# Levels 1 and 3 cross attention of a four-level Perceiver: scores stored negated by the operation that finds their maximum, turned probabilities of a unit in two banks

## The chip, the cores and the metric

The kernel is one program on one core of a Trainium2 chip. The time is what the device takes for one execution, in microseconds (us). The core has TensorE (PE; its weight loads are listed as PEld), VectorE (DVE), ScalarE (ACT), GpSimd (POOL) and SyncE (SP), each with its own queue of instructions; they wait for each other by semaphores. Matrix products write to PSUM, which the kernel divides into eight banks of 128 x 512 numbers of 4 bytes. Everything here is in float32.

## What is computed

The reference runs four levels over `x` (2 batches of 64 rows, 256 features). Each level has a cross attention to a context of 2 x 1024 rows with 192 features, a second mixing block, and a mixture of experts. The change is in the cross attention of levels 1 and 3, which have the same core (level 3 goes on with a two-layer product instead of `Wo`):

```python
q = (query @ Wq + bq).reshape(B, Nq, NUM_HEADS, HEAD_DIM).transpose(0, 2, 1, 3)
k = (key @ Wk + bk).reshape(B, Nk, NUM_HEADS, HEAD_DIM).transpose(0, 2, 1, 3)
v = (value @ Wv + bv).reshape(B, Nk, NUM_HEADS, HEAD_DIM).transpose(0, 2, 1, 3)
attn = jnp.einsum('bhqd,bhkd->bhqk', q, k) * SCALE
attn = jax.nn.softmax(attn, axis=-1)
out = jnp.einsum('bhqk,bhkd->bhqd', attn, v)
```

Here B = 2, Nq = 64, Nk = 1024, 16 heads of 16 features. The query is the normalized `x`, so each level's attention waits for everything before it; keys and values come from the context and are made ahead.

## The kernel before

The program goes level by level. `narrow_attention` (L1277) does the attention of levels 1 and 3. Its work is cut into 16 **units**. A unit is one batch `b`, one half `c` of the features (8 heads) and one pair `t` of heads: its scores have 128 rows (2 heads x 64 queries) and 1024 columns (keys). Four units with the same `b` and `c` make a **group** `g`. The function walks through 8 **rounds** `r` of two units, `mine = 2r` and `other = 2r + 1`.

A unit goes through these steps:

- `scores` (L1307): four products in all for the two units of a round; each unit's scores fill two neighbouring PSUM banks (`two_banks`).
- `largest` (L1320): DVE finds the negated maximum of each row (L1322), straight from PSUM.
- `exponentials` (L1324): ACT computes exp(score - maximum) from PSUM into the SBUF tile `p` and sums each row (L1328).
- `turn` (L1333): PE transposes `p`, four blocks of 128 x 128 for each half `k` of the keys (L1343), into one bank.
- `take` (L1349): the bank is copied to the SBUF tile `pT`, by ACT (L1352) or DVE (L1354). Of the four banks of a round, ACT takes three and DVE the last.
- `weigh` (L1364): for the group before, PE multiplies V with the turned probabilities of all four units, the half `k` = 0 in even rounds and 1 in odd ones (L1369); in even rounds it also transposes the reciprocal row sums, which DVE (`rinv`, L1359) and POOL (`wide`, L1361) have spread.
- `first_half`, `second_half`, `heads_of`: DVE takes the product out of its bank (`part`, L1381 and L1386), POOL masks it, and DVE scales it and puts the two heads together (`own`, `n_oT`).

Two things set when a step can run. First, the whole stage stands under `in_written_order` (L274): PE, DVE, ACT and POOL each run their instructions in the order in which the function writes them. Second, there are few buffers. PSUM is split by `psum(3, 2)`: three pairs of banks, from which `two_banks()` hands out one, and two single banks, from which `bank()` does. A new tile waits until the last reader of the buffer that it gets is done. Before the change, pairs hold scores only, and are free when the exponential has read them; single banks hold turned probabilities and the product of `weigh`, five uses in a round. `p` has three buffers, `pT` one or two for each of the eight pieces of a group.

The part of a round that is rewritten is this (L1415 to L1428):

```python
exponentials(other)
if more:
    scores(r + 1)
ps = turn(mine, 0)
take(mine, 0, ps, nc.scalar)
ps = turn(mine, 1)
if more:
    largest(mine + 2)
take(mine, 1, ps, nc.scalar)
if g >= 0:
    po = weigh(g, k, wide)
if more:
    exponentials(mine + 2)
```

After it come `turn(other, 0)`, `largest(other + 2)`, the half of `part`, the two copies of `other` and, in odd rounds, `heads_of`. Before the loop, the stage makes the queries, the scores of units 0 and 1, the last pieces of the keys, and the first maxima and the first exponential. After it, the last group is multiplied.

Of the kernel before, what the change touches and what calls it, by code (L numbers as in the profile page):

```python
# [8 lines left out]
F32 = mybir.dt.float32  # L9
U8 = mybir.dt.uint8  # L10
U32 = mybir.dt.uint32
AF = mybir.ActivationFunctionType
ALU = mybir.AluOpType
AX = mybir.AxisListType
# [3 lines left out]
P = 128  # L18
# [3 lines left out]
NK = 1024  # L22
# [35 lines left out]
def tile_perceiver(ctx: ExitStack, tc: tile.TileContext, i: dict, out: bass.AP):  # L58
    nc = tc.nc
# [30 lines left out]
    def two_banks():  # L90
        return psum_now["a"].tile([P, 1024], F32, tag="a", name="two_banks")

    def stat(n=1, name="stat"):
        return small.tile([P, n], F32, tag=f"s{n}", bufs=12 if n == 1 else 4, name=name)

    turn = [0]
# [65 lines left out]
    ident = const.tile([P, P], F32, name="ident")  # L162
# [640 lines left out]
    with psum(2, 4), stage_pool(name="l0x", bufs=1) as pool, stage_pool(  # L803
        name="l0x_prep", bufs=2
# [189 lines left out]
        sc, p, rinv, pT, u, uT = {}, {}, {}, {}, {}, {}  # L994
# [84 lines left out]
        ps = bank()  # L1079
# [28 lines left out]
        a, b, c, d = ((b, j) for b in range(NB) for j in range(2))  # L1108
# [165 lines left out]

    def narrow_attention(pool, att, x, wq, bq, bv, kv, gap, tail=()):  # L1277
        qx = pool.tile([P, 2, 2, NB, 2, S], F32, name="n_qx")
        oT = pool.tile([P, 2, P], F32, name="n_oT")
        kT, v = kv.kT, kv.v  # L1280
        bq_own = stat(8, "bq_own")
        at = COL[bq][0]
        for h in range(2):
            nc.vector.tensor_scalar(
                bq_own[:, 4 * h : 4 * h + 4], cols[:, at : at + 4], quarter[:, h : h + 1],
                None, ALU.mult,
            )
        units = [(b, c, t) for b in range(NB) for c in range(2) for t in range(4)]
        rounds = len(units) // 2
        sc, p, total, pT, part = {}, {}, {}, {}, {}  # L1290

        def queries(ps, c):

            for n in range(2):
                for h in range(2):
                    dst = qx[:, c, n, :, h, :]
                    src = ps[:, n * P : (n + 1) * P].rearrange("p (b q) -> p b q", b=NB)
                    one, k = quarter[:, h : h + 1], 2 * c + n
                    if n == 0:
                        nc.vector.tensor_scalar(dst, src, col(bq, k), one, ALU.add, ALU.mult)  # L1300
                    else:
                        nc.scalar.activation(
                            dst, src, AF.Identity, bias=bq_own[:, 4 * h + k : 4 * h + k + 1],
                            scale=one,
                        )

        def scores(r):  # L1307
            for u in (2 * r, 2 * r + 1):
                b, c, t = units[u]
                sc[u] = two_banks()  # L1310
                for n in range(2):
                    rows_ = 32 * ((t + 2 * n) % 4)
                    rows_ = slice(rows_, rows_ + 32)
                    nc.tensor.matmul(  # L1314
                        sc[u][:, n * 512 : (n + 1) * 512],
                        qx[rows_, c, n, b].rearrange("p h q -> p (h q)"), kT[c, b][rows_, n, :],
                        start=True, stop=True,
                    )

        def largest(u):  # L1320
            sc[u] = sc[u], stat(name="negmax")
            nc.vector.tensor_reduce(sc[u][1], sc[u][0], AX.X, ALU.max, negate=True)  # L1322

        def exponentials(u):  # L1324
            if u % 4 == 0:
                total[u // 4] = stat(4, "total")
            p[u] = att.tile([P, NK], F32, tag="p", name="p")
            nc.scalar.activation(  # L1328
                p[u], sc[u][0], AF.Exp, bias=sc[u][1], scale=1.0,
                accum_out=total[u // 4][:, u % 4 : u % 4 + 1],  # L1330
            )

        def turn(u, k):  # L1333


            t = u % 4
            pT[u, k] = att.tile(
                [P, 4, P], F32, tag=f"pT{t}{k}", bufs=1 if 2 * k + 1 <= t else 2,
                name="pT",
            )  # L1340
            ps = bank()
            for kc in range(4):
                nc.tensor.transpose(  # L1343
                    ps[:, kc * P : (kc + 1) * P],
                    p[u][:, (4 * k + kc) * P : (4 * k + kc + 1) * P], ident,
                )
            return ps

        def take(u, k, ps, engine):  # L1349
            dst = pT[u, k].rearrange("p c t -> p (c t)")  # L1350
            if engine is nc.scalar:
                nc.scalar.copy(dst, ps)  # L1352
            else:
                nc.vector.tensor_copy(dst, ps)  # L1354

        def spread(g):

            rinv = stat(4, "rinv")
            nc.vector.reciprocal(rinv, total[g])  # L1359
            wide = att.tile([P, 4, 32], F32, tag="wide", bufs=2, name="wide")  # L1360
            nc.gpsimd.tensor_copy(wide, rinv.unsqueeze(2).to_broadcast([P, 4, 32]))  # L1361
            return wide

        def weigh(g, k, wide=None):  # L1364
            b, c, _ = units[4 * g]
            po = bank()
            for kc in range(4 * k, 4 * k + 4):
                for t in range(4):
                    nc.tensor.matmul(  # L1369
                        po[32 * t : 32 * t + 32, :P],  # L1370
                        v[:, b, kc // 4, kc % 4, c * P + 32 * t : c * P + 32 * t + 32],
                        pT[4 * g + t, k][:, kc % 4, :], start=(kc == 4 * k), stop=(kc == 4 * k + 3),
                    )
            if k == 0:

                nc.tensor.transpose(po[:, P : 2 * P], wide.rearrange("p t d -> p (t d)"), ident)
            return po

        def first_half(g, po):
            part[g] = att.tile([P, 2 * P], F32, tag="part", bufs=2, name="part")  # L1380
            nc.vector.tensor_copy(part[g], po[:, : 2 * P])  # L1381
            own = part[g][:, P:]
            nc.gpsimd.tensor_tensor(own, own, parity, ALU.mult)

        def second_half(g, po):
            nc.vector.tensor_tensor(part[g][:, :P], po[:, :P], part[g][:, :P], ALU.add)  # L1386

        def heads_of(g):
            b, c, _ = units[4 * g]
            own = att.tile([P, P], F32, tag="own", bufs=2, name="own")  # L1390
            nc.vector.tensor_tensor(own, part[g][:, :P], part[g][:, P:], ALU.mult)

            nc.vector.scalar_tensor_tensor(
                oT[:, c, b * S : (b + 1) * S], own[:, :S], col(bv, c), own[:, S:],
                ALU.add, ALU.add,
            )

        with in_written_order():
            steps(gap, 3)
            xlT = turned_rows(layernorm(x, then=AF.Exp))  # L1400
            ps = [features(xlT, wq, 2 * c, 2) for c in range(2)]
            queries(ps[0], 0)
            scores(0)
            queries(ps[1], 1)
            steps(gap)
            largest(0)
            exponentials(0)
            largest(1)
            for r in range(rounds):
                g, k = r // 2 - 1, r % 2  # L1410
                mine, other = 2 * r, 2 * r + 1
                more = r + 1 < rounds
                if g >= 0 and k == 0:
                    wide = spread(g)
                exponentials(other)  # L1415
                if more:
                    scores(r + 1)
                ps = turn(mine, 0)
                take(mine, 0, ps, nc.scalar)
                ps = turn(mine, 1)  # L1420
                if more:
                    largest(mine + 2)
                take(mine, 1, ps, nc.scalar)
                if g >= 0:
                    po = weigh(g, k, wide)
                if more:
                    exponentials(mine + 2)
                ps = turn(other, 0)  # L1428
                if more:
                    largest(other + 2)  # L1430
                if g >= 0:
                    (second_half if k else first_half)(g, po)
                take(other, 0, ps, nc.scalar)
                ps = turn(other, 1)
                take(other, 1, ps, nc.vector)
                if g >= 0 and k:
                    heads_of(g)
            g = rounds // 2 - 1
            wide = spread(g)
            first_half(g, weigh(g, 0, wide))  # L1440
            second_half(g, weigh(g, 1))
            steps(tail, 1)
            heads_of(g)
            steps(tail)
        return oT
# [931 lines left out]
```

## Time and profile before

The time is 718.98 us, the median of three runs (718.66 to 720.44).

| what | value |
|---|---|
| span of the profiled execution | 719.9 us |
| time of the profiled execution | 721.7 us |
| granted PE clock over it, mean | 0.976 |
| PE busy | 663.7 us (92%) |
| PEld busy | 514.3 us (71%) |
| DVE busy | 300.7 us (42%) |
| ACT busy | 262.4 us (36%) |
| POOL busy | 65.6 us (9%) |
| L1343, transposes of `p`: 256 of them | 39.7 us busy |
| L1322, maxima: 32 | 37.6 us busy, 1216 ns each |
| L1328, exponentials: 32 | 36.1 us busy, 1127 ns each |
| L1352, copies by ACT: 48 | 27.0 us busy, 588 ns each |
| level 1 attention, first scores to the last step of `n_oT` | 151.7 to 198.0 us |
| level 3 attention, the same | 577.7 to 622.6 us |

In the rows of the profile, a line such as L1343 is the kernel's line, then come the engine, the operation, the tile written and the tiles read, the shape as partitions x elements, and how often. Times are from the start of the span. What stands in brackets, or behind the second bar, is how long the engine sat idle before, and what ended that. The clock is the share of full speed that TensorE was granted.

### The profile page before, as it was taken

How to read it: one execution, taken by the hardware profiler on the slowest of the kernel's cores; microseconds unless marked ns; L12 is line 12 of the kernel's file. 1: busy time of each engine (PE TensorE's matmuls, PEld its weight loads, DVE VectorE, ACT ScalarE, POOL GpSimd, SP SyncE). 2: the span in 40 equal slices, each digit the busy share in tenths (PEclk: the TensorE clock that was granted, in tenths of full speed). 3: DMA queues.
4: the chain of work that ended last, by engine and by line, in shares of the span. 5: the costliest groups of instructions: out<-in, count | busy, mean ns of one | idle time of the engine just before them, and what ended most of it. 6: DMA issues, size and time to landing. Idle time of an engine off the chain costs nothing.

```text
span 719.9 us, 11877 instructions
## 1 busy us (share of the span) xinstructions
PE 663.7 (92%) x4916; PEld 514.3 (71%) x4916; DVE 300.7 (42%) x757; ACT 262.4 (36%) x541; POOL 65.6 (9%) x93
## 2 busy tenths in 40 slices
PE   7789979989979999999998989999999989779997
PEld 3456657955659998899997678999979856543543
DVE  5854443147650003555553435534331367543111
ACT  2453252258653242322222415305131278432111
POOL 3520100000100000000000030220000000000240
PEclk9999999989999999999999999999999999969999
DMA  9940011850005887100000400020148800447981
GB/s 285 422 170 1 1 51 54 307 195 1 2 2 189 302 284 278 59 1 2 1 1 30 147 0 1 3 80 39 59 150 305 301 5 2 162 204 283 376 335 66
DMA packets 21226, 92.81 MB, mean 129 GB/s; under 512 B 3043, under 2 KB 7669, under 8 KB 12373
## 3 DMA queue, kind: packets, MB, share of 16 engines
q1 hardware_dynamic: 18896, 85.70, 32.7%
q0 software_dynamic: 2016, 6.30, 2.4%
q8 instruction: 39, 0.64, 0.4%
q14 instruction: 15, 0.12, 0.0%
q10 hardware_dynamic: 260, 0.06, 0.0%
HBM read 98.20 MB, written 0.13 MB: 137 GB/s over the span
## 4 chain that ended last, share of the span: by engine, by line
PE 84%; DVE 9%; ACT 4%; issue 2%; DMA 0%; POOL 0%; DVEq 0%; ACTq 0%; POOLq 0%
PE bank L261 29%; PE bank L1642 6%; PE two_banks L590 5%; PE two_banks L1591 4%; PE bank L1343 4%; PE two_banks L1314 3%; PE bank L635 3%; PE two_banks L1598 2%; PE bank L1369 2%; PE two_banks L1837 2%; PE bank L1957 2%; PE two_banks L405 1%; PE two_banks L379 1%; PE two_banks L261 1%; PE bank L1945 1%
## 5 line engine op out<-in xcount | busy, mean ns | idle before, releaser
L1642 PE MATMUL bank<-l2x_ctx,p 128*128 128x193 f32 x256 | 48.1, 327 | 0.0
L354 DVE SCALAR_TENSOR_TENSOR x_new<-bank,comb,x_new 128x256 f32<-128x256 f32 x24 | 11.6, 484 | 79.7 <-PE bank L261 79.7
L1343 PEld LDWEIGHTS bank<-ident,p 128*128 128x128 f32 x256 | 29.9, 150 | 18.5 <-issue 7.8
L1642 PEld LDWEIGHTS bank<-l2x_ctx,p 128*128 128x128 f32 x256 | 40.8, 191 | 0.4
L1343 PE MATMUL bank<-ident,p 128*128 128x128 f32 x256 | 39.7, 299 | 1.3 <-ACT pT L1352 0.5
L1322 DVE TENSOR_REDUCE negmax<-two_banks 128x1 f32<-128x1024 f32 x32 | 37.6, 1216 | 7.2 <-PE two_banks L1314 7.2
L1328 ACT ACTIVATE p<-two_banks,negmax 128x1024 f32<-128x1024 f32 x32 | 36.1, 1127 | 0.8 <-DVE negmax L1322 0.8
L1352 ACT COPY pT<-bank 128x512 f32<-128x512 f32 x48 | 27.0, 588 | 14.6 <-PE bank L1343 14.6
L1591 PE MATMUL two_banks<-l2x_qA,ctxA 128*128 128x128 f32 x256 | 31.9, 278 | 0.0
L261 PEld LDWEIGHTS bank<-xT,l1f_w_sb 128*128 128x128 f32 x256 | 31.3, 201 | 0.6 <-issue 0.3
L261 PE MATMUL bank<-xT,l1f_w_sb 128*128 128x128 f32 x256 | 31.7, 285 | 0.0
L1591 PEld LDWEIGHTS two_banks<-l2x_qA,ctxA 128*128 128x128 f32 x256 | 30.3, 192 | 1.1 <-issue 1.0
L1532 ACT ACTIVATE l1f_hT<-bank,cols 128x128 f32<-128x128 f32 x64 | 18.3, 368 | 34.4 <-PE bank L261 34.4
L1606 DVE TENSOR_REDUCE l2x_mx<-two_banks 128x128 f32<-128x1024 f32 x16 | 19.6, 1225 | 26.5 <-PE two_banks L1598 26.5
L261 PEld LDWEIGHTS bank<-xT,l2f_w_sb 128*128 128x128 f32 x256 | 29.6, 192 | 0.3
L261 PE MATMUL bank<-xT,l2f_w_sb 128*128 128x128 f32 x256 | 29.8, 275 | 0.0
L261 PE MATMUL bank<-l1f_w_sb,l1f_hT 128*128 128x256 f32 x128 | 28.8, 379 | 0.0
L1314 PE MATMUL two_banks<-n_kT,n_qx 32*128 32x512 f32 x128 | 25.1, 677 | 2.8 <-ACT n_kT L450 1.8
L1628 DVE TENSOR_TENSOR p<-two_banks,l2x_shift 128x512 f32<-128x512 f32 x32 | 20.6, 687 | 13.1 <-ACT l2x_shift L1623 13.1
L261 PEld LDWEIGHTS bank<-l1f_w_sb,l1f_hT 128*128 128x128 f32 x128 | 23.8, 190 | 2.9
L1635 ACT ACTIVATE p<-p 128x512 f32<-128x512 f32 x32 | 19.6, 630 | 12.1 <-DVE p L1628 12.1
L590 PE MATMUL two_banks<-l3f_w_sb,m_xg 128*64 128x512 f32 (+1 forms) x112 | 23.0, 629 | 0.5 <-ACT m_xg L613 0.5
(565 smaller groups left out, 1296.8 us busy)
## 6 DMA issues: line engine op xcount, KB each, us to landing
l1f_w_sb<-in_l1f_w_dram SPq DMA_DIRECT2D x16, 1024.0 KB, 4.8
l3f_w_sb<-in_l3f_w_dram SPq DMA_DIRECT2D x12, 1024.0 KB, 7.7
more_w<-in_l3f_w_dram SPq DMA_DIRECT2D x12, 1024.0 KB, 11.9
l0f_w_sb<-in_l0f_w_dram SPq DMA_DIRECT2D x8, 1024.0 KB, 8.4
l2f_w_sb<-in_l2f_w_dram SPq DMA_DIRECT2D x8, 1024.0 KB, 4.7
l2f_w_sb<-in_l2f_w_dram SPq DMA_DIRECT2D x8, 512.0 KB, 6.5
xh<-in_ctx_dram SPq DMA_DIRECT2D x8, 192.0 KB, 5.6
l2x_ctx<-in_ctx_dram SPq DMA_DIRECT2D x1, 1536.0 KB
```

The costliest lines, as they stand in the source:

```text
L261: nc.tensor.matmul(dst, lhsT, rhs, start=(k == 0), stop=(k == len(pairs) - 1))
L590: nc.tensor.matmul(part[s], xg[r][:, c, s], shelf.at[r, j, n](c, f), start=False, stop=(c == 1), skip_group_check=True,)
L635: nc.tensor.matmul(ps[s, :D], hT[r][:, f, s], shelf.at[r, j, 2](f, slice(0, D)), start=(f == 0), stop=(f == last),)
L1314: nc.tensor.matmul(sc[u][:, n * 512 : (n + 1) * 512], qx[rows_, c, n, b].rearrange("p h q -> p (h q)"), kT[c, b][rows_, n, :], start=True, ...
L1322: nc.vector.tensor_reduce(sc[u][1], sc[u][0], AX.X, ALU.max, negate=True)
L1328: nc.scalar.activation(p[u], sc[u][0], AF.Exp, bias=sc[u][1], scale=1.0, accum_out=total[u // 4][:, u % 4 : u % 4 + 1],)
L1343: nc.tensor.transpose(ps[:, kc * P : (kc + 1) * P], p[u][:, (4 * k + kc) * P : (4 * k + kc + 1) * P], ident,)
L1352: nc.scalar.copy(dst, ps)
L1591: nc.tensor.matmul(sc[k][:, n, t, :], ctxA[:, b, n, t * P : (t + 1) * P], qA[:, j, b].rearrange("p h q -> p (h q)"), start=(t == 0), stop= ...
L1606: nc.vector.tensor_reduce(mx[k], sc[k].rearrange("p n t q -> p q (n t)"), AX.X, ALU.max)
L1628: nc.vector.tensor_tensor(p[k][:, n], sc[k][:, n], shifts[k].unsqueeze(1).to_broadcast([P, 4, P]), ALU.add,)
L1642: nc.tensor.matmul(po[k][:, : CD + 1], p[k][:, kc // 4, kc % 4, :], crows[:, b * 8 + kc, :], start=(kc == 0), stop=(kc == 7),)
```

## The change

The maximum becomes a minimum of the negated scores: one DVE operation reads the scores from PSUM, adds `zero` (a [128, 1] tile repeated along the row), multiplies by -1, stores the result in `p`, and reduces it by the minimum. It is two instructions, the operation and a read of the accumulator. The exponential then works in `p`, in place, with scale -1. `p` is taken at the maximum instead of at the exponential.

The transposes of the first unit of a round (`mine`) now fill a pair of banks, all eight blocks, and ACT copies the pair at once. Pairs of banks therefore hold scores and turned probabilities, and single banks the product and the other unit's two halves. The order within a round is changed: `largest(mine + 2)` is written before the transposes, `part` is taken right after the product, and `largest(other + 2)` follows behind `part`. `part` and `own` have one buffer each instead of two.

```diff
+        zero = stat(name="zero")
+        nc.vector.memset(zero, 0.0)
...
         def largest(u):
-            sc[u] = sc[u], stat(name="negmax")
-            nc.vector.tensor_reduce(sc[u][1], sc[u][0], AX.X, ALU.max, negate=True)
+            p[u] = att.tile([P, NK], F32, tag="p", name="p")
+            least = stat(name="negmax")
+            nc.vector.tensor_tensor_reduce(
+                p[u], sc[u], zero.to_broadcast([P, NK]), -1.0, 3.0e38, ALU.add, ALU.min, least
+            )
+            sc[u] = least
 
         def exponentials(u):
             if u % 4 == 0:
                 total[u // 4] = stat(4, "total")
-            p[u] = att.tile([P, NK], F32, tag="p", name="p")
             nc.scalar.activation(
-                p[u], sc[u][0], AF.Exp, bias=sc[u][1], scale=1.0,
+                p[u], p[u], AF.Exp, bias=sc[u], scale=-1.0,
                 accum_out=total[u // 4][:, u % 4 : u % 4 + 1],
             )
+
+        def turn_into(ps, u, k):
+            for kc in range(4):
+                nc.tensor.transpose(
+                    ps[:, kc * P : (kc + 1) * P],
+                    p[u][:, (4 * k + kc) * P : (4 * k + kc + 1) * P], ident,
+                )
...
+        def turn_all(u):
+            whole = att.tile([P, 2, 4, P], F32, tag=f"pT{u % 4}", bufs=2, name="pT")
+            ps = two_banks()
+            for k in range(2):
+                pT[u, k] = whole[:, k]
+                turn_into(ps[:, k * 512 : (k + 1) * 512], u, k)
+            nc.scalar.copy(whole.rearrange("p k c t -> p (k c t)"), ps)
...
-            part[g] = att.tile([P, 2 * P], F32, tag="part", bufs=2, name="part")
+            part[g] = att.tile([P, 2 * P], F32, tag="part", bufs=1, name="part")
...
-            own = att.tile([P, P], F32, tag="own", bufs=2, name="own")
+            own = att.tile([P, P], F32, tag="own", bufs=1, name="own")
...
                 exponentials(other)
                 if more:
                     scores(r + 1)
-                ps = turn(mine, 0)
-                take(mine, 0, ps, nc.scalar)
-                ps = turn(mine, 1)
-                if more:
                     largest(mine + 2)
-                take(mine, 1, ps, nc.scalar)
+                turn_all(mine)
                 if g >= 0:
                     po = weigh(g, k, wide)
+                    (second_half if k else first_half)(g, po)
                 if more:
                     exponentials(mine + 2)
+                    largest(other + 2)
                 ps = turn(other, 0)
-                if more:
-                    largest(other + 2)
-                if g >= 0:
-                    (second_half if k else first_half)(g, po)
                 take(other, 0, ps, nc.scalar)
                 ps = turn(other, 1)
                 take(other, 1, ps, nc.vector)
```

More of the change, by code (lines that the diff above doesn't have):

```diff
@@ L1341, in turn @@
             ps = bank()
[L1342 to L1346, printed above, removed]
-            return ps
+            turn_into(ps, u, k)
+            return ps
+        def turn_all(u):
[5 more added lines that the diff above has]
+            nc.scalar.copy(whole.rearrange("p k c t -> p (k c t)"), ps)
         def take(u, k, ps, engine):
```

## The prediction

> **What bounds the kernel now.** I first read the page's list of costliest groups to find the two cross attentions: the 256 transposes of L1343, the 32 maxima of L1322, the 32 exponentials of L1328. They run at 151.7 to 199 us (level 1) and 577.7 to 623 us (level 3); the rest of the program is not touched. Then the busy time by stretches, whose columns are: us, busy PE, PEld, DVE, ACT, POOL (with counts), granted PE clock, DMA share, GB/s.
>
> ```profile
> 158.00:162.00 4.00, 4.00 (x22) 3.21 (x22) 1.32 (x2) 2.48 (x5) 0.00 (x0) 0.50 0.00 0
> ...
> 171.40:180.70 9.30, 8.74 (x114) 5.73 (x113) 7.27 (x11) 7.72 (x15) 0.74 (x2) 1.00 0.01 2
> ```
>
> In the steady part (second line, two rounds) TensorE is busy 94% of the time, at full clock; ACT 83%, DVE 78%. Much cannot be won there. The first line is the opening, two rounds in which the clock stands at half. What stops TensorE in the steady part is in the waits of PE, 163 to 196 us (us in total, times, longest):
>
> ```profile
> PE bank L1369 <- ACT pT L1352: 1.4, 6, 0.2
> PE bank L1376 <- POOL wide L1361: 0.5, 1, 0.5
> ```
>
> Six times the product with V (L1369) waits for ScalarE's copy of turned probabilities (L1352). The timeline of a pair of rounds shows where:
>
> ```profile
> 171.39 1.14 PE L1314 MATMUL two_banks<-n_kT,n_qx 32*128 32x512 f32 x8
> ...
> 172.46 1.09 PE L1343 MATMUL bank<-ident,p 128*128 128x128 f32 x8
> ...
> 173.16 1.07 ACT L1352 COPY pT<-bank 128x512 f32<-128x512 f32 x2 [0.70 <-PE bank L1343]
> ...
> 173.79 1.08 PE L1369 MATMUL bank<-pT,n_v 128*32 128x128 f32 x32 [0.24 <-ACT pT L1352]
> 174.12 1.13 ACT L1328 ACTIVATE p<-two_banks,negmax 128x1024 f32<-128x1024 f32 x1
> 174.80 0.91 PEld L1343 LDWEIGHTS bank<-ident,p 128*128 128x128 f32 x8 [0.20 <-issue]
> ```
>
> Start to start: scores to transposes 1.07, transposes of the first unit to L1369 1.33, L1369 to the other transposes 1.02, these to the next scores 1.07 (at 175.88): 4.49 us. The next round (to 180.72) is 4.84: again 1.33, and 0.17 for the turned `wide` and 0.19 for a bank that `part` holds. The product takes its bank from the pair that the two transposes of the first unit have just used, so it waits for ScalarE to empty that bank. The product's inputs are a group old and long there.
>
> **The change, part by part.** The waits below are those of the changed program's own order.
>
> *Maximum, DVE, 32 times.* TENSOR_REDUCE 128x1024 (1216 ns) goes; an operation with two inputs, a stored output and an accumulator comes, and a read of the accumulator. No row shows this operation. Nearest rows:
>
> ```profile
> L1911 DVE SCALAR_TENSOR_TENSOR ns_junk<-bank,kqk 128x128 f32<-128x128 f32 x4 | 1.2, 292 | 1.1 <-ACT ns_n L1909 1.1
> L1911 DVE DVE_READ_ACCUMULATOR ns_junk<-bank,kqk 128x1 f32 x4 | 0.3, 84 | 0.0
> ...
> L942 DVE TENSOR_TENSOR kq<-kq,rn 128x1024 f32<-128x1024 f32 x4 | 4.9, 1233 | 0.1
> L2035 DVE TENSOR_TENSOR s<-two_banks,s 128x1024 f32<-128x1024 f32 x2 | 2.5, 1225 | 10.1 <-PE two_banks L1845 6.2 <-PE two_banks L261 3.9
> ```
>
> L2035 has the size with scores' memory as one input (1225), L942 an input repeated over 64 elements, much as `zero` is (1233), L1911 has the accumulator (84 for the read; its 292 equals the plain two-input L1953 at 291). So 1.23 + 0.08 = 1.31, or 1.26 start to start where the reduces stand 1.18 apart: +0.08 each. [...] I take 1.31[...]. The cheap end is 1.22, a plain reduce.
>
> *Exponential, ACT, 32 times.* It reads `p` in SBUF instead of PSUM. L1635, an exponential on SBUF, takes 630 for 512 elements, the PSUM copy of 512 588: +0.04, so 1.17 for 1.13. Two banks of scores now come free at the maximum, not at the exponential.
>
> *Copies, ACT.* Two copies of 512 (0.48 apart) become one of 1024. ACT's slope is (1127 - 588)/512 with unlike operations, so at most 1.05 ns; a copy of 1024 lies between 0.95 (two pitches) and 1.13: I take 1.0. ACT per round: 2 x 1.17 + 1.0 + 0.48 = 3.8 of 4.4 us. No more than before within 0.1.
>
> *Banks.* The pair that the first unit's transposes fill is a two-bank slot, which waits for the maximum of the previous round's other unit, not for ScalarE. The product's bank now comes from copies of the round before. So 1.33 becomes 1.07: **0.26 a round**.
>
> *Order on DVE.* `part` moves ahead of the second maximum, so that maximum now stands behind an instruction that waits for the product. Behind it: the next round's first transposes (slot) and the exponential. Even round, from the product's start: 1.01 + 0.36 (`wide` until `part` starts) + 0.42 + 1.26 + 0.08 = 3.13; PE comes to those transposes after 1.01 + 0.17 + 1.26 + 1.07 = 3.51. Covered by 0.38. Odd: 1.15 + 0.29 + 1.34 = 2.78 against 3.16. The cover falls at a maximum of some 1.6 us. DVE in two rounds: 4 x 1.26 + 2.8 = 7.9 of 8.8. The third `p` buffer: taken at the maximum, it waits for transposes that stand before the product; covered by the same product. `part` and `own` with one buffer: reader and next writer are a round apart on the same engine. `zero`: one memset of [128,1], during the gate of level 0 and beside matmuls. DMA issues and their queues keep their order.
>
> *Steady sum.* Rounds 2 to 6: 5 x 0.26 = 1.3. In the last round the unit turned in 1.59 (614.63 to 616.22, second half waiting for a bank of L1354) takes 1.07: 0.5. **1.8 per level.** The tail after the last product waits for `rinv` and `wide` as before.
>
> *Opening* (rounds 0 and 1). Before, the second unit's scores wait for an exponential (582.24 for 580.61) and T(0) starts at 583.34. After, they wait for maxima, and the chain is ScalarE's: exp(0) 581.0 to 582.25, exp(1) to 583.4, copy to 584.5, exp(2) to 585.7, copy 586.2, exp(3) 587.4, copy 588.4, exp(4) 589.6. The transposes of round 2 start at 589.7 for 592.19: 2.5. But the clock: at 583.3 to 586.9 it reads 0.54, and at 158 to 162 0.50. [...] (3.3 us at half in level 3, about 6.8 in level 1, where the opening is 15.9 us against 14.5). With the halves where they are now, T(1) and the scores behind it end 0.8 later: 1.7 remain in level 3, and 1.0 in level 1 (166.6 for 167.61). [...] with no half window, 2.5 and 3.9. I take the row.
>
> *Sum.* 2 x 1.8 + 1.7 + 1.0 = 6.3. The profiled execution is 721.7 us around its span of 719.9, and goes to 715.4; the median of the runs shown is 718.98, 2.7 under it, so **712.7 us**.
>
> **Rivals.**
> 1. *Opening hidden.* The clock's half windows or ScalarE's chain eat its gain; the steady 3.6 stay: 715.4. For it: ACT is the chain there, with equal work. Against: scores no longer wait for exponentials.
> 2. *More.* No half window in either opening: 3.6 + 2.5 + 3.9 = 10.0, 709.0. [...]
> 3. *No change.* The 0.24 moves to another bank, such as `part`'s: 718. Against: the changed program's product waits only for older copies.
> 4. *The maximum is dear: slower.* DVE carries 2.8 / 2 = 1.4 us per round beside two maxima. It is the bound from (4.4 - 1.4)/2 = 1.5 us, and loses against today's 4.67 from 1.62. [...] For it: the operation has no row of its own. Against: the four rows above.
>
> **Numbers.** Forecast 0.66, opening hidden 0.13, more 0.06, no change 0.06, dear maximum 0.09. Range 707.5 to 717.5: it takes the first three cases and leaves out the dear maximum and part of no change. 0.3% is 2.2 us, about what a measurement of this kernel tells from nothing: faster 0.84, same 0.07, slower 0.09.
>
> **What would show it.** Right: the maximum's row near 1.23 us with a read of 84 ns; no wait of the product for the copy; a pair of rounds 8.8 us for 9.33; T(0) a microsecond earlier. Wrong: a maximum over 1.5 us; first transposes waiting for DVE; exponentials over 1.2.

## The result, and the profile after

The changed kernel takes 711.02 us, the median of four runs (706.28 to 714.86), where the kernel before took 719.71 on the same chip (718.66 to 721.47): a ratio of 0.987 (95% interval 0.983 to 0.992). The profiled execution took 714.86 us around a span of 713.2, at a mean granted clock of 0.971; before it was 721.7 us, 719.9 and 0.976. The two profiles differ by 6.8 us, the medians by 8.7.

The page's list of costliest groups has the new maximum and the exponential, both 32 times; the last columns are us busy, mean ns, and idle time ahead of them:

```profile
L1327 DVE CUSTOM_DVE_ANT_0 p<-two_banks,zero 128x1024 f32<-128x1024 f32 x32 | 38.8, 1217 | 7.5 <-PE two_banks L1317 4.1
...
L1335 ACT ACTIVATE p<-p,negmax 128x1024 f32<-128x1024 f32 x32 | 37.0, 1155 | 1.7 <-DVE negmax L1327 1.6
```

The maximum that also stores 1024 numbers costs what the plain one cost (1217 ns for 1216), and the exponential 28 ns more. Two smaller groups, from the list with shapes kept apart, are the read of the accumulator and ScalarE's copy of a whole unit:

```profile
L1365 ACT COPY pT<-two_banks 128x1024 f32<-128x1024 f32 x16 | 16.2, 1010 | 6.2 <-PE two_banks L1342 6.2
...
L1327 DVE DVE_READ_ACCUMULATOR2_ANT negmax<- 128x1 f32 x32 | 2.6, 83 | 0.0
```

These are the waits of PE from 163 to 196 us (us in total, times, longest):

```profile
PE bank L1342 <- ACT p L1335: 0.5, 1, 0.5
PE bank L1394 <- POOL wide L1379: 0.5, 1, 0.5
PE bank L1387 <- ACT pT L1370: 0.2, 1, 0.2
```

The six waits of the product for ScalarE's copy are gone. What is left stands outside the steady rounds: one in the opening, two behind the last round. The timeline of a steady round (start, us, engine, line):

```profile
168.99 1.14 PE L1317 MATMUL two_banks<-n_kT,n_qx 32*128 32x512 f32 x8
...
170.06 1.09 PE L1342 MATMUL two_banks<-ident,p 128*128 128x128 f32 x8
170.27 1.23 DVE L1327 CUSTOM_DVE_ANT_0 p<-two_banks,zero 128x1024 f32<-128x1024 f32 x1 [0.18 <-PE two_banks L1317]
...
171.08 1.08 PE L1387 MATMUL bank<-pT,n_v 128*32 128x128 f32 x32
171.19 1.01 ACT L1365 COPY pT<-two_banks 128x1024 f32<-128x1024 f32 x1 [0.43 <-PE two_banks L1342]
171.42 0.08 DVE L1327 DVE_READ_ACCUMULATOR2_ANT negmax<- 128x1 f32 x1
172.09 1.14 PE L1342 MATMUL bank<-ident,p 128*128 128x128 f32 x8
```

From the first transposes to the product it is now 1.02 us (before 1.33), although ScalarE begins its copy only when the product is already running. The busy time by stretches of the opening and of a pair of rounds (us; busy PE, PEld, DVE, ACT, POOL; granted clock; DMA):

```profile
155.00:159.00 4.00, 3.61 (x14) 2.01 (x15) 3.11 (x6) 2.72 (x5) 0.00 (x0) 0.61 0.09 35
...
168.99:177.70 8.71, 8.63 (x114) 5.74 (x113) 7.12 (x16) 7.87 (x14) 0.74 (x2) 1.00 0.01 2
```

TensorE is busy 99% of a steady pair, for 94% before. The pair itself, from scores to scores, takes 8.71 us (168.99 to 177.70) where it took 9.33.

Where the time went, from the timelines of both profiles. An attention is counted from its first scores to the first product that waits for the last of `n_oT`, its opening from the first scores to the transposes of round 2:

| stretch | before | after | gain |
|---|---|---|---|
| level 1, opening | 15.90 | 13.08 | 2.82 |
| level 1, the rest | 30.96 | 28.72 | 2.24 |
| level 3, opening | 14.53 | 13.00 | 1.53 |
| level 3, the rest | 30.51 | 28.37 | 2.14 |
| ahead of level 1, and between the levels | 530.80 | 530.26 | 0.54 |
| behind level 3 | 97.2 | 99.7 | -2.5 |

The six gains make 6.8, the difference of the spans. In level 1's opening part of the gain is the clock's: it stood at half for 6.8 us there before, for 3.4 after (in level 3's for 3.4 both times). The last row is work that the change does not touch. After the change it ran longer because TensorE stood at half clock for 20 us there (14 before); the time at half is summed from the granted clock in stretches of 3.4 us.

### The profile page after: what moved, and what is told of

It is laid out like the page before. It is cut to its first block, busy times and chain, and to the rows that moved or that the text cites. A ratio compares the mean times of both kernels' runs of the same rounds, so it can differ in the third digit from the quotient of the medians.

```text
span 713.2 us, 11917 instructions
## 1 busy us (share of the span) xinstructions
PE 661.2 (93%) x4916; PEld 513.5 (72%) x4916; DVE 300.3 (42%) x791; ACT 260.9 (37%) x525; POOL 65.7 (9%) x93
## 4 chain that ended last, share of the span: by engine, by line
PE 86%; DVE 8%; ACT 4%; issue 2%; DMA 0%; POOL 0%; ACTq 0%; DVEq 0%; POOLq 0%
PE bank L261 29%; PE bank L1654 6%; PE two_banks L590 5%; PE two_banks L1603 4%; PE bank L635 3%; PE two_banks L1610 2%; PE two_banks L379 2%; PE two_banks L1342 2%; PE two_banks L1317 2%; PE two_banks L1849 2%; PE bank L1387 2%; PE bank L1342 2%; PE bank L1969 2%; PE two_banks L405 1%; PE two_banks L381 1%
## 5 line engine op out<-in xcount | busy, mean ns | idle before, releaser
L1327 DVE CUSTOM_DVE_ANT_0 p<-two_banks,zero 128x1024 f32<-128x1024 f32 x32 | 38.8, 1217 | 7.5 <-PE two_banks L1317 4.1
L1335 ACT ACTIVATE p<-p,negmax 128x1024 f32<-128x1024 f32 x32 | 37.0, 1155 | 1.7 <-DVE negmax L1327 1.6
L261 PEld LDWEIGHTS bank<-xT,l1f_w_sb 128*128 128x128 f32 x256 | 29.7, 192 | 0.6 <-issue 0.3
L261 PE MATMUL bank<-xT,l1f_w_sb 128*128 128x128 f32 x256 | 30.1, 276 | 0.0
L1317 PE MATMUL two_banks<-n_kT,n_qx 32*128 32x512 f32 x128 | 22.9, 678 | 1.8 <-ACT n_kT L450 1.8
L1342 PEld LDWEIGHTS two_banks<-ident,p 128*128 128x128 f32 x128 | 15.1, 151 | 12.4 <-ACT p L1335 6.1
L214 ACT ACT_TABLE_LOAD x16 | 20.5, 1283 | 0.3
L1342 PE MATMUL bank<-ident,p 128*128 128x128 f32 x128 | 18.8, 282 | 1.5 <-ACT p L1335 1.0
```

Of the source, the lines that this page charges most:

```text
L214: nc.scalar.activation(junk, behind, func, scale=0.0)
L261: nc.tensor.matmul(dst, lhsT, rhs, start=(k == 0), stop=(k == len(pairs) - 1))
L1317: nc.tensor.matmul(sc[u][:, n * 512 : (n + 1) * 512], qx[rows_, c, n, b].rearrange("p h q -> p (h q)"), kT[c, b][rows_, n, :], start=True, ...
L1327: nc.vector.tensor_tensor_reduce(p[u], sc[u], zero.to_broadcast([P, NK]), -1.0, 3.0e38, ALU.add, ALU.min, least)
L1335: nc.scalar.activation(p[u], p[u], AF.Exp, bias=sc[u], scale=-1.0, accum_out=total[u // 4][:, u % 4 : u % 4 + 1],)
L1342: nc.tensor.transpose(ps[:, kc * P : (kc + 1) * P], p[u][:, (4 * k + kc) * P : (4 * k + kc + 1) * P], ident,)
```

## The experiments

My theory was that of the prediction: the steady gain comes from the product's bank, the rest from scores that come free at the maximum, and the maximum is beside other work until DVE is full. The rivals: one half of the change does it alone, the order on DVE does it, or the maximum sits on the path. Every experiment was timed beside the kernel before, on the same chip.

**The changed kernel again.** Its spread in the result was wide, so it ran once more, beside the first experiments.

> The changed kernel once more. Level times, from the first scores to the first product that follows the attention: 41.8 us (level 1) and 41.4 us (level 3) in its first profile, against 46.9 and 45.0 before. My theory: a pair of steady rounds is again 8.7 us for 9.33, since nothing in it hangs on the run; the opening of a level (first scores to the transposes of round 2, 13.1 and 13.0 us) moves by one or two us with the half-clock windows, and so does the whole time, by about 0.45 us for each us at half clock. Rival: the gain itself varies from run to run, and the pair of rounds moves by over 0.1 us.

710.72 us (709.52 to 712.07), ratio 0.988 (0.985 to 0.992). The gain stands. In this profile neither opening had a half window (3.4 us in which the granted clock reads 0.50, as from 583.2 to 586.6 before the change): both took 11.7 us, and the attentions 40.37 and 40.04. The pair was 8.71 again.

**The maximum alone.** The kernel before, with the new maximum and the exponential from `p`; banks and order as they were.

```diff
 def largest(u):
-    nc.vector.tensor_reduce(sc[u][1], sc[u][0], AX.X, ALU.max, negate=True)
+    p[u] = att.tile([P, NK], F32, tag="p", name="p")
+    nc.vector.tensor_tensor_reduce(p[u], sc[u], zero.to_broadcast([P, NK]),
+        -1.0, 3.0e38, ALU.add, ALU.min, least)
...
```

> Only the maximum and the exponential are changed; the transposes, copies, banks and the order of a round are those of before. My theory: the product's wait for ScalarE's copy stays (0.24 us, six times a level), a pair of steady rounds stays within 9.2 to 9.5 us, and only the opening gains, 1 to 2 us a level, since scores no longer wait for an exponential. Rival (the maximum with its store is the whole change): pairs fall to 8.7 us and the levels to some 41.5 us.

717.96 us, ratio 0.998 (0.996 to 0.9995). The longest of its waits of PE, same window:

```profile
PE bank L1375 <- ACT pT L1358: 1.7, 6, 0.5
```

This is the product's wait, undiminished (1.4 before), and the pair takes 9.35. All that this half brings is in the openings: 12.10 in both levels, without a half window, where the changed kernel has 11.7 without one. How much of the gain over 15.90 and 14.53 is the clock's is not shown, since no profile has the openings of the kernel before at full clock. This half frees the scores' banks at the maximum, but in the steady part nobody was waiting for those.

**Banks and order alone.** The changed kernel with the plain maximum, so that the exponential reads PSUM and holds the pair of banks until it is done.

```diff
 def largest(u):
-    nc.vector.tensor_tensor_reduce(p[u], sc[u], zero.to_broadcast([P, NK]),
-        -1.0, 3.0e38, ALU.add, ALU.min, least)
+    nc.vector.tensor_reduce(sc[u][1], sc[u][0], AX.X, ALU.max, negate=True)
...
```

> Only the banks and the order are changed; the maximum is the plain reduce and the exponential reads PSUM. My theory: the product's wait for the copy is gone, but the first transposes of a round now take the pair of banks that the other unit's exponential has to free, and wait 0.3 to 0.6 us for it each round; a pair of rounds is 8.9 to 9.6 us, the opening is longer than the changed kernel's by 1 us or more (the first transposes wait for the second exponential), a level 43.5 to 46.5 us. Rival (the banks are the whole change): pairs of 8.7 us, levels of 41.5 us.

726.27 us, ratio 1.009 (1.006 to 1.012): slower than the kernel before. Its longest waits of PE:

```profile
PE two_banks L1336 <- ACT p L1329: 3.2, 6, 0.7
PE bank L1381 <- ACT pT L1364: 0.2, 1, 0.2
```

The product's steady wait is gone here too. In its place the first transposes (L1336) wait for the exponential, since the pair of banks that they fill still holds scores: 0.70 and 0.52 in a pair of rounds, which takes 10.26, and the levels take 49.0 and 48.6: the wait is the one I had named, and it costs more than I had expected. So the two halves are one change. Alone they move the time by -0.2% and +0.9%, together by -1.2% (the repeat, on the same chip): three pairs of banks serve scores and turned probabilities only if scores leave them at the maximum.

**The order on DVE.** The changed kernel with `part` behind the second maximum again, as in the kernel before.

```diff
 po = weigh(g, k, wide)
-(second_half if k else first_half)(g, po)
 ...
 largest(other + 2)
+(second_half if k else first_half)(g, po)
```

> The changed kernel with the second maximum ahead of part again, as before the change. My theory: part then starts when the second maximum is done. In even rounds the second maximum ends some 2.5 us after the first started, at about the time at which part starts now, so 0 to 0.2 us are lost there by the bank that part holds; in odd rounds, 0 to 0.2. A pair of rounds 8.7 to 9.0 us: the order is worth little. Rival (the order is what makes the change work): pairs of 9.1 us or more.

709.99 us (708.13 to 710.52), ratio 0.987 (0.984 to 0.991): no slower in the whole. Two of the waits of PE, same window, tell more:

```profile
PE bank L1342 <- DVE part L1399: 0.4, 2, 0.2
PE bank L1342 <- DVE part L1404: 0.3, 2, 0.2
```

The other unit's transposes wait for the single bank that `part` holds, 0.15 and 0.19 us each time, a pair takes 9.15 and the attentions 41.23 and 40.80: 1.6 us longer than in the run of the changed kernel beside it. That run stood at half clock for about 31 us of its profile and this one for about 24 (2 x (1 - mean clock) x span, from 0.978 and 0.983), which offsets it. So the order is worth 0.44 of the 0.62 us that a pair gains, a little more than my theory allowed (9.0 for the pair) and just past the rival's 9.1: with `part` taken late, the wait moves on to the bank that `part` holds. The openings, at 11.7 in both levels here too, don't depend on it.

**More work on DVE at every maximum, twice.** The changed kernel with one more maximum over 192 or 512 of the columns behind each, whose result nobody reads.

```diff
     least)
+nc.vector.tensor_reduce(stat(name="spare"), sc[u][:, :192], AX.X, ALU.max)
```

> The changed kernel with one more maximum over 192 columns of the same scores behind every maximum, whose result nobody reads: each maximum dearer by about 0.3 us (1.21 to about 1.55 start to start). My theory: VectorE has that room, the two maxima of a round are 3.1 of its work beside 1.4 of partial sums, 4.5 us a round, against 4.36 now, so the steady pair of rounds goes from 8.71 to 9.0 to 9.2 and the level's attention grows by about 2 us (half of it in the openings, where each maximum is on the path): some 714 to 716 in all, still faster than before. Rival one, the dear maximum of the prediction (the chain scores, maximum, exp, transposes runs through each maximum with no cover): every maximum's 0.3 shows, pair 9.9, 10 us over both levels, about 720. Rival two (full cover): pair 8.71, 711 to 712.

> The same with 512 columns more, each maximum dearer by about 0.65 us (1.87 start to start). My theory: VectorE sets the pace, 2 x 1.87 + 1.4 = 5.1 us a round, pair 10.2 to 10.5, against 9.33 in the kernel before: 12 us over both levels against the changed kernel and slower than before, 722 to 727. Rival (the maximum is mostly beside other work): pair at most 9.3, 715 or less.

With 192 columns 711.06 us, ratio 0.990 (0.988 to 0.993); with 512, 718.87 us, ratio 1.000 (0.998 to 1.001). The busy time of a pair of rounds, first with 192 columns, then with 512:

```profile
169.49:178.20 8.71, 8.63 (x114) 5.74 (x114) 8.10 (x20) 7.87 (x15) 0.74 (x2) 1.00 0.01 2
```

```profile
170.78:180.10 9.32, 8.72 (x114) 5.75 (x113) 9.28 (x20) 7.79 (x13) 0.75 (x2) 1.00 0.01 2
```

With 192 columns DVE goes from 7.12 to 8.10 us and the pair stays at 8.71: full cover in the steady rounds, as the second rival had it, and my 9.0 to 9.2 was wrong. (In level 3's opening, at full clock in both runs, 0.46 us show: 12.13 for 11.67.) With 512 DVE is busy 9.28 of 9.32 and sets the pace, as the theory has it, but at 9.32 and not above 10, and the whole takes 718.87 and not 722 or more. Both misses have one cause, my prices. On the timeline a maximum takes 1.14 us from its start to the next instruction's, 1.41 with 192 columns and about 1.73 with 512 (I had 1.21, 1.55 and 1.87), and the rest of DVE's work is (9.32 - 4 x 1.73) / 2 = 1.2 us a round, not 1.4. By an estimate from these, DVE becomes the bound at (8.71 - 2.4) / 4 = 1.58 us (no run lies between 1.41 and 1.73), and the steady gain over the kernel before is lost at (9.33 - 2.4) / 4 = 1.73, which is where the second run stands.

These two runs load DVE and hold the scores' banks longer, but they do not lengthen the way from a maximum to its exponential. The timeline with 192 columns:

```profile
168.76 1.22 DVE L1327 CUSTOM_DVE_ANT_0 p<-two_banks,zero 128x1024 f32<-128x1024 f32 x1
...
169.90 0.08 DVE L1327 DVE_READ_ACCUMULATOR2_ANT negmax<- 128x1 f32 x1
169.90 0.35 DVE L1330 TENSOR_REDUCE spare<-two_banks 128x1 f32<-128x192 f32 x1
170.02 1.15 ACT L1336 ACTIVATE p<-p,negmax 128x1024 f32<-128x1024 f32 x1
```

The exponential starts at 170.02, beside the added maximum. A maximum that is itself dearer would delay it too. The exponential ends at 171.17 and PE comes to the transposes that read it at 172.59, which suggests room for that, but no run shows it; the rival of the dear maximum is answered for DVE's time, and for the rest by the measured 1217 ns.

**Idle work against the half clock.** The question is whether the half clock goes when TensorE's gaps there are filled. Transposes of the identity into a spare bank, read by nobody: six between the first two score blocks and four ahead of the first transposes, then in addition sixteen in the block behind level 3's attention.

```diff
 steps(gap)
+spare = bank(); idle_work(spare, 6)
 largest(0)
...
 scores(r + 1)
+if r == 0:
+    idle_work(spare, 4)
...
 nc.scalar.mul(less_sums, ps[:, :8], -1.0)
+idle_work(bank(), 16)
```

> The changed kernel with idle TensorE work in both openings: six transposes of the identity between the first two score blocks and four ahead of the first unit's transposes, read by nobody. My theory: [...] with the gaps filled no opening has one, both take about 11.7 us (13.0 with one window), and the kernel is 0 to 2.5 us faster by the median, with the granted clock at full from the first scores to round 2. Rival one: the windows don't depend on these gaps; openings of 11.7 and 13.0 as before by chance, the same time. Rival two: the idle work itself delays the scores, openings of 12.0 or more at full clock, 0.5 to 1 us slower.

> As the run with idle work in the openings, and 16 more idle transposes of the identity in the block behind level 3's attention, where TensorE stands still for 2.6 us ahead of the block's products and the granted clock was at half for 20 us of the profiled run. My theory: [...] with it filled the time at half clock in the 25 us behind level 3's attention falls from 20 us to under 7, and the kernel is faster by about 0.45 us for each, 3 to 6 us, 704 to 708. Rival: the clock there is held down by what came before (or by chance), and the time is that of the run without these 16, within 1 us.

The first took 710.13 us (708.63 to 711.21), ratio 0.989 (0.987 to 0.990). Its openings ran at full clock and took 11.88 us, 0.2 more than in the repeat, which had no half window either without any idle work. So this run cannot tell whether the idle work kept the windows out. (Of the six openings in the three profiles of the changed kernel with idle work none has one; of six without, in the first profile, the repeat and the order's run, two have. That is too few to tell.) The second took 707.27 us (706.69 to 708.30), ratio 0.984 (0.983 to 0.986), the fastest of all. The stretch from 612 to 640 us, without and with the sixteen transposes:

```profile
612.00:640.00 28.00, 20.71 (x86) 10.95 (x84) 9.77 (x40) 9.38 (x18) 1.04 (x1) 0.70 0.55 218
```

```profile
612.00:640.00 28.00, 21.92 (x118) 13.02 (x118) 10.59 (x42) 10.24 (x20) 1.04 (x1) 0.82 0.59 241
```

The clock goes from 0.70 to 0.82 there: 10 us at half instead of 17, not under 7 as I had it, and 2.9 us less by the medians. One pair of profiles could be chance: the run with 192 columns stood at half for 10 us there without any idle work. But the executions do not overlap, with mean clocks of 0.978 to 0.981 without the sixteen and 0.983 to 0.985 with them, and times of 708.63 or more and 708.30 or less. The gain is shown, and that it comes by way of the clock is likely.

**The same idle work in the kernel before, and more of it in the changed one** (twelve transposes behind the routers' products of the block that follows).

> The kernel before, with the idle TensorE work of the last run: six and four transposes of the identity in both openings, sixteen in the block behind level 3's attention. It separates what the change is worth from what the clock adds: both kernels now have openings and block at full clock. My theory: a level's attention takes about 43 us (12.1 of opening without a half window, as in the run with the maximum alone, and steady pairs of 9.33), against 40.2 to 40.4, so 5.4 us over both levels lie between it and the changed kernel with the same idle work (707.27): 712 to 714.5, and 4.5 to 7 us below the kernel before. Rival: the idle work does nothing for this kernel, whose gaps are longer; openings of 14.5 to 16 and 717 to 720.

> The run with idle work in the openings and behind level 3's attention, and twelve more idle transposes behind the routers' products of the block that follows (1.88 us of standstill ahead of the products with the triangular matrix; the 10 us at half clock that were left lay from 622 on, around this standstill). My theory: that half-clock time goes or is halved, and the kernel gains another 2 to 4 us: 703 to 705.5. Rival: [...] the time stays at 706.5 to 708.

The kernel before with idle work takes 716.26 us, ratio 0.995 (0.993 to 0.996). That is 4.0 below the kernel before on that chip, between my 712 to 714.5 and the rival's 717 to 720. Its openings still had one half window each (level 1's had two before) and took 14.95 and 15.10 us, as the rival said. What causes the windows stays open. But its rounds behind the opening took 30.95 and 30.51 us, against 28.71 and 28.37 with the change and the same idle work: the 2.24 and 2.14 of the table again, to the hundredth. The spans of these two profiles, whose mean clocks are 0.987 and 0.985, differ by 9.3 us: 4.4 in these rounds, 6.3 in the openings, where one had half windows and the other none, and 1.4 the other way elsewhere. The twelve further transposes brought nothing (708.38, ratio 0.984, 0.982 to 0.986): I had expected 2 to 4 us. In both runs the half clock began at 622.8, two microseconds ahead of the gap that they fill, and ended at 633.

## Why the prediction was right

Its forecast, 712.7, lies 1.7 above the median, and the mechanism that it named for the steady rounds is the one that the runs show. The size was short: a gain of 6.3 was forecast, and 8.7 was measured by the medians (8.2 in the repeat), nearer to the 10.0 of rival 2. By its steps:

- **The product's wait.** Right: it is gone, and no wait has taken its place in the steady part. I had 1.33 falling to 1.07; it fell to 1.02, and the pair is 8.71, not 8.81. That the bank was the reason is shown from two sides: with the maximum alone the wait stays, with the banks alone it goes.
- **The steady sum** was mis-sized: 1.8 per level, measured 2.24 and 2.14. The step as I put it gave the new order on DVE no worth, only a cover to keep, and gave the whole gain to the banks; the run without the order showed that the wait would otherwise go to `part`'s bank, as rival 3 had it, for most of the gain (0.44 of 0.62). Two pairs of 0.62 make 1.24 where I had 1.04; the remaining 0.9 to 1.0 is round 6 and the end, where I had 0.76.
- **The maximum.** The size was right: 1217 ns and 83 for the read, forecast 1230 and 84. Start to start it was 1.14, below the 1.26 I took. The dear maximum of rival 4 does not appear: with the scores read from PSUM and `zero` from SBUF, the operation took 1217 ns where the plain maximum took 1216. No run has that operation with its sources placed otherwise.
- **Exponential and copy.** 1.155 for 1.17, and 1.01 for 1.0.
- **The cover on DVE.** I had it fall at a maximum of 1.6, the bound at 1.5 and the loss from 1.62. The runs with added columns put the bound at some 1.58 and the loss at 1.73, for DVE's time alone. The term that was off is DVE's other work, 1.2 a round and not 1.4.
- **The opening.** In level 3, with one half window in both profiles, it gained 1.53 for the 1.7 forecast. In level 1 it gained 2.82, where I had 1.0. I had kept the two half windows of the profile before; only one came back, and the repeat had none. For openings without a half window I had 2.5 and 3.9; the repeat gained 2.9 in level 3 and 4.2 in level 1. T(0), the start of the first transposes, came 0.6 us earlier in level 3's profile (5.08 for 5.68 after the first scores), and 1.06 earlier in the repeat, at full clock.
- **The sum.** 6.3 forecast, 8.7 over both attentions in the profiles, of which 2.5 went back behind level 3, where the clock stood lower; 6.8 in the profiled executions. That these 6.8 come so near to the 6.3 is luck: the steps were short by 2.4, and a stretch that the change does not touch took as much away. Rival 2, more, supposed no half window in either opening. The repeat's profile shows that state: its two attentions are 11.5 us shorter than those before, and its span is 707.7. Over its runs the gain was 8.2 (710.72 against 718.92), so it seems that the windows fall in some executions and not in others, and the gain by the medians lies between the forecast's case and that rival's. The steady part, 4.4 of it, is the same in every profile of the changed kernel; the rest moves with the clock, and how much of it is the change's own stays open.

## What to carry to other kernels

When a product waits for a bank, look at which engine empties that bank and when, then look for another slot that comes free earlier; a change that frees one buffer sooner may pay only together with the one that puts other work into it (here -0.2% and +0.9% alone, -1.2% together). Price added work on an engine by the time from its start to the next instruction's (here 1.14 us for a row of 1217 ns), and work out from the busy time of a pair of rounds at which price that engine becomes the bound. Compare such versions stage by stage and at equal clock: here the same program had openings of level 1 of 13.1 us with one half window and 11.7 without, and these 1.4 us are about what the change gained in level 3's opening (1.53).

## What the hardware did that was not expected

Most of the spread goes with the time at half clock. The four runs of the changed kernel have spans from 713.2 to 704.6 us at mean clocks of 0.971 and 0.984: (1 - clock) / 0.5 x span is 41.4 us at half in the first and 22.5 in the last, so 8.6 us of span for 18.9, about 0.45 us for each. The same program had 13.1 us openings in one profile and 11.7 in another. The stretches at half in the profiles before and after each lasted 3.4, 6.8, 10.2 or 20.5 us. TensorE's busy time just ahead does not tell where the clock falls: in the 3.4 us ahead of the half clock in level 3's opening before the change (579.8 to 583.2) TensorE was busy for 2.09, but for only 1.93 of another 3.4 us of the same profile (49.0 to 52.4), and the clock stayed full through them and the 3.4 us behind them.

In the last experiment TensorE was busy 90% or more of every microsecond from 624 to 628, inside the half-clock stretch behind level 3 (us; busy PE, PEld, DVE, ACT, POOL; granted clock; DMA):

```profile
624.00:625.00 1.00, 0.90 (x5) 0.90 (x5) 0.53 (x3) 1.00 (x1) 0.00 (x0) 0.50 1.09 459
625.00:626.00 1.00, 1.00 (x6) 1.00 (x7) 0.74 (x5) 0.29 (x2) 0.00 (x0) 0.50 1.00 426
626.00:627.00 1.00, 1.00 (x7) 1.00 (x6) 0.82 (x5) 0.04 (x1) 0.00 (x0) 0.50 0.63 262
627.00:628.00 1.00, 1.00 (x7) 1.00 (x6) 0.00 (x0) 0.16 (x1) 0.00 (x0) 0.50 0.04 16
```

The clock came back at 633, 10.2 us after it fell at 622.8. What brings the half clock, and what ends it, these runs don't tell.
